# A unit's result turned in eight pieces on VectorE and laid out through DRAM, and the maxima's rounding two exponentials later

## The chip, the cores and the metric

The kernel runs on one core of a Trainium2 chip. The metric is the device time of one execution in microseconds. An execution taken with the hardware profiler gives the trace that the prediction reads; its times are counted from the start of the profiled span.

## The reference

One transformer layer: attention with 16 heads over 4096 tokens of width 256, then a gated feed-forward part, each followed by a residual sum and a layer norm. The change concerns the attention alone:

```python
B, N, d = x.shape            # 1, 4096, 256
h = H                        # 16
dk = d // h                  # 16
proj = quant4(x) @ ternary_weight(Wqkv_w).T + Wqkv_b
q = proj.reshape(B, N, h, dk).transpose(0, 2, 1, 3)
k = proj.reshape(B, h, N, dk)
v = proj.reshape(B, h, N, dk)
q, k = (rotary(q, N), rotary(k, N))
ql, kl = (q @ U, k @ U)
att = jnp.einsum('bhnr,bhmr->bhnm', ql, kl) / math.sqrt(dk)
y = jax.nn.softmax(att, axis=-1) @ v
y = y.transpose(0, 2, 1, 3).reshape(B, N, d)
return quant4(y) @ ternary_weight(Wo_w).T
```

## The kernel before, in words

**Units and steps.** The attention is cut into 64 units. A unit is a pair of heads and a block of 512 queries; the 4096 keys are passed in 32 tiles of 128, one tile to a step. The softmax needs the largest score of every query before any exponential, so each unit is gone through twice: first `largest` (L468 to L486) multiplies queries with keys and keeps only maxima, and 40 steps later (`LAG` = 32 + 8) `weights` (L511 to L519) multiplies again, with the maximum subtracted by a first matmul of `minus` and `m_rows`, and takes the exponential on ScalarE. `values` (L533) multiplies the exponentials of two steps with the values, in eight matmuls, four column strips of 32 running together, into the PSUM tile `av` of 128 x 512: per head of the pair two strips, one for even and one for odd key tiles, each with 16 value columns and one column that sums the exponentials. So in any step one unit's maxima, another's exponentials and a third's values are worked on side by side.

**The order.** Instructions stand in the order in which the program emits them; each engine and each DMA queue takes its own in that order. A loop over steps `s` first calls what was registered for the step with `at(step, f)`, then for odd `s` `largest(s)` and `weights(s - LAG)`, for even `s` `weights(s - LAG)` and `largest(s)`. `values` comes at odd steps, ahead of `largest`. On TensorE a pair of steps is therefore: eight `av` matmuls, two L468 matmuls, four score matmuls (L511), four more, two L468 matmuls.

**PSUM.** `ps_1` has three banks of 128 x 512. Each step of `largest` takes two of them, and VectorE frees each with one reduction of 512 columns (L476). Every other small use takes a bank of the same three: the turning of the queries (`query_steps`, L439), the preparing of the keys (L361, L367, L393), the projections (L139, L147), and the turning of a finished unit (L553). The scores have two double banks (`ps_sc`), `av` has one.

**A unit's maxima.** At a unit's last step of `largest`, VectorE reduces the 128 x 64 collected maxima to `m` (L481), ScalarE rounds them to a first part (L485) and GpSimd subtracts for the second (L486), all emitted inside `largest`, ahead of `weights` of the same step. Two steps on, `largest_rows` turns them on VectorE (L492), stores them to `m_dram` (L497) and loads them as rows (L500), both on SP's queue. They are needed when the unit's exponentials begin. Counted from the unit's first step of `largest`, its last is step 31, the turning step 34, the first exponential step 40.

**A unit's end.** `finish(u, 0)` copies `av` to SBUF on ScalarE (L548). Four steps later `finish(u, 1)` turns it in four fp32 transposes on TensorE into a `ps_1` bank (L553), VectorE adds the two strips of each head (L557), takes the reciprocal of the sums (L564), multiplies (L566), and SP stores the 512 x 32 result to `y_dram` (L572). After the last unit the feed-forward stage begins; its first VectorE operation (L737) splits the turned tokens, and its weights `h2` and `w3` are loaded on GpSimd's queue, emitted after the loop of steps.

GpSimd prepares queries and keys (L329 to L334, L431, L432), and from the ninth unit on rounds the weights for a check (L594, L595).

Of the kernel before, what the change touches and what calls it, by code (L numbers as in the profile page):

```python
# [9 lines left out]
F32 = mybir.dt.float32  # L10
# [4 lines left out]
ALU = mybir.AluOpType  # L15
AX = mybir.AxisListType
PSUM = bass.MemoryType.PSUM

P = 128
# [3 lines left out]
DK = D // H  # L23
HALF = DK // 2
NT = N // P
QB = 512
NQB = N // QB
NKT = N // P
DH = 1024
NC = DH // P  # L30
BT = 4
# [6 lines left out]
def attn_ffn_kernel(  # L38
# [22 lines left out]
    nc = tc.nc  # L61
# [6 lines left out]
    ident = const.tile([P, P], F32, name="ident")  # L68
# [11 lines left out]
    dram = ctx.enter_context(tc.tile_pool(name="dram", bufs=1, space=bass.MemoryType.DRAM))  # L80
# [157 lines left out]
    with ExitStack() as actx:  # L238
# [16 lines left out]
        m_parts = big.tile([P, 2, 2, 2, BT], F32R, name="m_parts")  # L255
        m_turned = big.tile([P, 32], F32, name="m_turned")
        m_rows = [big.tile([P, QB], F32R, name=f"m_rows{i}") for i in range(2)]
        m_dram = [dram.tile([32, P], F32, name=f"m_dram{i}") for i in range(2)]

        qpool = actx.enter_context(tc.tile_pool(name="qpool", bufs=2))  # L260
# [3 lines left out]
        ps_1 = actx.enter_context(tc.tile_pool(name="ps_1", bufs=3, space=PSUM))  # L264
# [185 lines left out]
        NU = (H // 2) * NQB  # L450
        LAG = NKT + 8
        AVLAG = 4
        kTs, qTs, mxs, avs, probs = {}, {}, {}, {}, {}
        todo = {}

        def at(step, f):
            todo.setdefault(step, []).append(f)

        def largest(s):

            u, i = divmod(s, NKT)
            qt, ck = divmod(i, NKT // BT)
            if i == 0:
                mxs[u] = stat.tile([P, BT, 2, NKT // BT], F32, name="mx")
            ps = [ps_1.tile([P, 512], F32, name="ps1") for j in range(2)]
            for j in range(2):
                rows = slice(64 * j, 64 * j + 64)
                nc.tensor.matmul(  # L468
                    ps[j],
                    lhsT=qTs[u][rows, ts(qt, P)],  # L470
                    rhs=kTs[u // NQB][rows, ts(ck, 512)],
                    start=True,
                    stop=True,
                )
            for j in range(2):
                nc.vector.tensor_reduce(  # L476
                    mxs[u][:, qt, j, ck : ck + 1], ps[j], AX.X, ALU.max
                )
            if i == NKT - 1:
                m = stat.tile([P, 2, BT], F32, name="m")  # L480
                nc.vector.tensor_reduce(  # L481
                    m, mxs.pop(u).rearrange("p t j c -> p j t c"), AX.X, ALU.max
                )
                parts = m_parts[:, 0]
                nc.scalar.copy(parts[:, :, 0, :], m)  # L485
                nc.gpsimd.tensor_tensor(  # L486
                    parts[:, :, 1, :], m, parts[:, :, 0, :].bitcast(F32), ALU.subtract
                )

        def largest_rows(u):  # L490

            nc.vector.transpose(  # L492
                m_turned, m_parts.bitcast(F32).rearrange("p a j k t -> p (a j k t)")
            )

            rows = m_dram[u % 2]
            nc.sync.dma_start(out=rows.rearrange("r (b c) -> b r c", b=4), in_=m_turned)  # L497
            rows = rows[: 4 * BT].rearrange("(j k t) c -> j k (t c)", j=2, k=2)
            for j in range(2):
                nc.sync.dma_start(  # L500
                    out=m_rows[u % 2][64 * j : 64 * j + 2, :].bitcast(F32), in_=rows[j]
                )
# [19 lines left out]
        def values(s):  # L522

            u, kt = divmod(s, NKT)
            pair = u // NQB
            if kt == 0:
                avs[u] = ps_av.tile([P, QB], F32, name="av")
            for j in range(2):
                for k in range(2):
                    a, c = divmod(kt + k, H)  # L530
                    strip = 32 * (2 * j + k)

                    nc.tensor.matmul(  # L533
                        avs[u][strip : strip + 32, :],
                        lhsT=v_all[
                            :, 2 * (2 * pair + j) + a, c * (DK + 1) : c * (DK + 1) + 32
                        ],
                        rhs=probs[s + k][:, j, :],
                        start=(kt == 0),
                        stop=(kt == NKT - 2),  # L540
                    )
            del probs[s], probs[s + 1]

        def finish(u, part, state={}):
            pair, qb = divmod(u, NQB)
            if part == 0:
                state[u] = qpool.tile([P, QB], F32, name="ya")
                nc.scalar.copy(state[u], avs.pop(u))  # L548
                return
            ya = state.pop(u)  # L550
            ps = ps_1.tile([P, 512], F32, name="ps1")
            for t in range(BT):
                nc.tensor.transpose(ps[:, ts(t, P)], ya[:, ts(t, P)], ident)  # L553

            both = ps.rearrange("p (n k e) -> p n k e", k=2, e=32)[:, :, :, : DK + 1]
            y = qpool.tile([P, BT, 2, DK + 1], F32, name="y")
            nc.vector.tensor_reduce(  # L557
                y.rearrange("p t j e -> p (t j) e"),
                both.rearrange("p n k e -> p n e k"),
                AX.X,  # L560
                ALU.add,
            )
            den = stat.tile([P, BT, 2], F32, name="den")
            nc.vector.reciprocal(den, y[:, :, :, DK])  # L564
            yu = stat.tile([P, BT, 2, DK], F32, name="yu")
            nc.vector.tensor_tensor(  # L566
                yu,
                y[:, :, :, :DK],
                den.unsqueeze(3).broadcast_to([P, BT, 2, DK]),
                ALU.mult,  # L570
            )
            nc.sync.dma_start(  # L572
                out=y_dram[qb].rearrange("(t p) d -> p t d", p=P)[
                    :, :, pair * 32 : (pair + 1) * 32
                ],
                in_=yu.rearrange("p t j e -> p t (j e)"),
            )
# [33 lines left out]
        with tc.manual_schedule():  # L611
# [32 lines left out]
            for u in range(NU):  # L644
                pair, qb = divmod(u, NQB)
                if qb == 2 and pair + 1 < H // 2:
                    def start_keys(pair=pair, u=u):
                        kTs[pair + 1] = kpool.tile([P, N], F32R, name="kT")
                        steps = key_steps(pair + 1, kTs[pair + 1])
                        for i, f in enumerate(steps):  # L650
                            at(NKT * u + 40 + 6 * i, f)
                    at(NKT * u + 8, start_keys)

                def start_queries(u=u, pair=pair, qb=qb):
                    qTs[u] = qpool.tile([P, QB], F32R, name="qT", bufs=3)
                    natural, transposed = query_steps(pair, qb, qTs[u])
                    natural()
                    at(NKT * (u - 1) + 26 if u else 0, transposed)

                if u:  # L660
                    at(NKT * (u - 1) + (18 if u == 1 else 6), start_queries)
                else:
                    start_queries()
                base = NKT * u + LAG
                for kt in range(0, NKT, 2):
                    at(base + kt + 1 + AVLAG, lambda s=NKT * u + kt: values(s))
                at(NKT * (u + 1) + 2, lambda u=u: largest_rows(u))
                at(base + NKT + AVLAG - 1, lambda u=u: finish(u, 0))
                at(base + NKT + AVLAG + 3, lambda u=u: finish(u, 1))
            last = NKT * NU  # L670
            at(last - 240, lambda: load_weights(w1_sb, w1T, 0))
            w2_sb, h1_sb, h2_sb = [None, None], [None, None], [None, None]
# [22 lines left out]
                    at(last + 2 + i, f)  # L695

            at(last - 60, start_front)
            for s in range(NKT * NU + LAG + AVLAG + 6):
                while todo.get(s):
                    todo[s].pop(0)()  # L700

                if s < NKT * NU and s % 2:
                    largest(s)
                if 0 <= s - LAG < NKT * NU:
                    weights(s - LAG)
                if s < NKT * NU and not s % 2:
                    largest(s)
# [213 lines left out]
```

## Time and profile before

| | |
|---|---|
| median of three executions | 3770.27 us (3770.03 to 3770.37) |
| profiled execution | 3770.6 us |
| its span, and granted TensorE clock | 3768.8 us, 0.988 |
| attention stage, about | 113 to 3088 us of the span |
| one unit in the steady stretch (1553.39 to 1598.81) | 45.42 us: TensorE busy 45.03, VectorE 41.14, ScalarE 32.90, GpSimd 6.54 |
| L476, reduction of 512 columns on VectorE | 4096 times, 684 ns recorded |
| L553, transposes of a unit on TensorE | 256 times, 286 ns |
| L557, L564, L566 on VectorE | 431, 204 and 292 ns, 64 times each |
| L485 on ScalarE, L486 on GpSimd | 197 and 206 ns, 64 times each |
| ScalarE's wait for `m` before L485 | 112.8 us in 64 times |

An engine's busy time is the union of what it ran; recorded durations of neighbours overlap, so that starts are closer together than durations say. An idle stretch is put down to the event that came last before it ended. The chain of waits is followed back from the last instruction to what released it each time; what does not stand on it had time to spare.

### The profile page before, as it was taken

To read this page: it belongs to the slowest core of one execution; us is meant where nothing else is said; L and a number is where in the kernel's file an instruction comes from. 1 tells how busy PE (TensorE), PEld (TensorE's weight loads), DVE (VectorE), ACT (ScalarE), POOL (GpSimd) and SP (SyncE) were. 2 spreads that over 40 slices of the span, in tenths; PEclk is the share of its full clock that TensorE was granted. 3 is DMA by queue.
4 is the path that set the end of the run, shared out by engine and by line. 5 is a ranking of instruction groups with operands and counts; after the bars stand their busy time and mean duration, and the time that the engine had idled before them with its cause. 6 is when DMAs were issued, how large, how long until landed. Compare 5 with 4: busy or idle time off the path is not lost.

```text
span 3768.8 us, 61593 instructions
## 1 busy us (share of the span) xinstructions
PE 3688.5 (98%) x24651; PEld 2065.1 (55%) x24651; DVE 3041.0 (81%) x5254; ACT 2381.5 (63%) x2782; POOL 471.5 (13%) x840
## 2 busy tenths in 40 slices
PE   6999999999999999999999999999999999999998
PEld 3454445444444454445444544455445448888887
DVE  6988988899889988998899889988999945555544
ACT  1566777777777777777777777767777773333333
POOL 3342112111211121111011111100000000000000
PEclk6999999999999999999999999999999999999999
DMA  1000000000000000000000000000010020000000
GB/s 36 13 14 3 9 9 9 9 9 9 9 9 9 9 9 9 9 9 8 9 9 9 9 9 9 9 3 3 25 48 14 9 70 6 18 17 24 28 6 13
DMA packets 78072, 50.91 MB, mean 14 GB/s; under 512 B 52688, under 2 KB 72400, under 8 KB 77776
## 3 DMA queue, kind: packets, MB, share of 16 engines
q1 hardware_dynamic: 73952, 35.35, 3.5%
q0 software_dynamic: 3824, 11.54, 0.9%
q8 instruction: 195, 3.19, 0.3%
q14 instruction: 101, 0.83, 0.1%
HBM read 37.44 MB, written 9.44 MB: 12 GB/s over the span
## 4 chain that ended last, share of the span: by engine, by line
PE 89%; DVE 6%; ACT 3%; issue 1%; POOL 0%; DMA 0%; ACTq 0%; SPq 0%
PE av L533 25%; PE sc L511 23%; PE ps L468 19%; PE ps_mm L753 17%; DVE mx L476 5%; ACT pr L519 2%; PE ps L553 1%; PE ps L393 1%; PE ps L439 1%; DVE m L481 0%; PE ps L367 0%; PE ps L361 0%; PE ps L147 0%; DVE ma L119 0%; PE ps_mm L798 0%
## 5 line engine op out<-in xcount | busy, mean ns | idle before, releaser
L476 DVE TENSOR_REDUCE mx<-ps 128x1 f32<-128x512 f32 x4096 | 2564.2, 684 | 308.4 <-PE ps L468 280.2
L519 ACT ACTIVATE pr<-sc 128x1024 f32<-128x1024 f32 x2048 | 2003.9, 1023 | 755.4 <-PE sc L511 743.7
L533 PE MATMUL av<-pr,v_all 128*32 128x512 f32 x8192 | 1092.0, 605 | 0.0
L468 PEld LDWEIGHTS ps<-kT,qT 64*128 64x128 f32 x4096 | 549.1, 185 | 972.1 <-DVE mx L476 699.1
L468 PE MATMUL ps<-kT,qT 64*128 64x512 f32 x4096 | 1047.7, 470 | 14.0 <-DVE mx L476 7.9
L511 PE MATMUL sc<-m_rows,minus 64*128 64x512 f32 x4096 | 851.6, 409 | 16.2 <-ACT pr L519 12.2
L511 PE MATMUL sc<-qT,kT 64*128 64x512 f32 x4096 | 815.0, 391 | 0.0
L511 PEld LDWEIGHTS sc<-m_rows,minus 64*128 64x128 f32 x4096 | 392.5, 185 | 134.4 <-ACT pr L519 84.8
L511 PEld LDWEIGHTS sc<-qT,kT 64*128 64x128 f32 x4096 | 393.2, 185 | 74.1
L533 PEld LDWEIGHTS av<-pr,v_all 128*32 128x32 f32 x8192 | 161.6, 108 | 267.9 <-issue 266.7
L486 POOL TENSOR_TENSOR m_parts<-m,m_parts 128x8 fp32r<-128x8 f32 x64 | 13.2, 206 | 2233.4 <-ACT m_parts L485 2233.4
L786 ACT ACTIVATE gate<-ps_mm,sc_hs 128x512 f32<-128x512 f32 x128 | 88.1, 688 | 312.8 <-PE ps_mm L753 269.6
L735 DVE CAST h<-gate 128x512 fp32r<-128x512 f32 x128 | 54.4, 425 | 223.1 <-ACT gate L786 223.1
L737 DVE TENSOR_TENSOR h<-gate,h 128x512 fp32r<-128x512 f32 x192 | 132.3, 689 | 5.1
L753 PE MATMUL ps_mm<-h,h1a 128*128 128x512 f32 x512 | 128.9, 394 | 0.0
L753 PE MATMUL ps_mm<-h,h2a 128*128 128x512 f32 x512 | 127.2, 391 | 0.0
L753 PE MATMUL ps_mm<-h,h1b 128*128 128x512 f32 x512 | 126.5, 389 | 0.0
L753 PE MATMUL ps_mm<-h,h2b 128*128 128x512 f32 x512 | 126.5, 389 | 0.0
L778 DVE SCALAR_TENSOR_TENSOR gate<-ps_mm,sc_s,gate 128x512 f32<-128x512 f32 x64 | 48.0, 750 | 81.9 <-ACT gate L776 58.0
L753 PEld LDWEIGHTS ps_mm<-h,h1b 128*128 128x128 f32 x512 | 96.1, 188 | 20.1
L753 PEld LDWEIGHTS ps_mm<-h,h2b 128*128 128x128 f32 x512 | 96.1, 188 | 19.9
L753 PEld LDWEIGHTS ps_mm<-h,h2a 128*128 128x128 f32 x512 | 95.6, 188 | 19.6
(148 smaller groups left out, 1915.4 us busy)
## 6 DMA issues: line engine op xcount, KB each, us to landing
xs<-in_x SPq DMA_DIRECT2D x16, 512.0 KB
y_dram<-yu SPq DMA_DIRECT2D x64, 64.0 KB
xs<-in_h1T SPq DMA_DIRECT2D x8, 512.0 KB
xs<-in_h2T SPq DMA_DIRECT2D x8, 512.0 KB
yb<-y_dram SPq DMA_DIRECT2D x8, 512.0 KB
out<-xs SPq DMA_DIRECT2D x8, 512.0 KB
m_rows<-m_dram SPq DMA_DIRECT2D x128, 4.0 KB
h1a<-in_h1T POOLq DMA_DIRECT2D x2, 1024.0 KB, 6.4
```

Of the source, the lines that this page charges most:

```text
L393: nc.tensor.matmul(ps[:, ts(k, P)], lhsT=flat[:, ts(4 * i + k, P)], rhs=identr, start=True, stop=True,)
L439: nc.tensor.matmul(ps[:, ts(t, P)], lhsT=qq[:, t].rearrange("p j k e -> p (j k e)"), rhs=identr, start=True, stop=True,)
L468: nc.tensor.matmul(ps[j], lhsT=qTs[u][rows, ts(qt, P)], rhs=kTs[u // NQB][rows, ts(ck, 512)], start=True, stop=True,)
L476: nc.vector.tensor_reduce(mxs[u][:, qt, j, ck : ck + 1], ps[j], AX.X, ALU.max)
L511: nc.tensor.matmul(ps[:, j, :], lhsT=minus[rows, :] if first else kTs[u // NQB][rows, ts(kt, P)], rhs=m_rows[u % 2][rows, :] if first else ...
L519: nc.scalar.activation(pr, ps, AF.Exp)
L533: nc.tensor.matmul(avs[u][strip : strip + 32, :], lhsT=v_all[:, 2 * (2 * pair + j) + a, c * (DK + 1) : c * (DK + 1) + 32], rhs=probs[s + k ...
L735: eng(dst[:, k, 0, :], g)
L737: nc.vector.tensor_tensor(dst[:, k, 1, :], g, dst[:, k, 0, :].bitcast(F32), ALU.subtract)
L753: nc.tensor.matmul(ps, lhsT=sb[:, ks, ts(o, P)] if split else wo[:, k, :], rhs=src[:, k, i, :], start=(k == 0 and i == 0), stop=(k == n - ...
L778: nc.vector.scalar_tensor_tensor(g, pb, scales["s2"][:, o : o + 1], gate, ALU.mult, ALU.mult)
L786: nc.scalar.activation(g, ps, AF.Gelu, scale=scales[sc][:, o : o + 1])
```

## The change

The four transposes on TensorE go. The copy of `av` is turned by VectorE instead, which transposes within blocks of 32 x 32: eight calls of 64 columns, one at every second step. Four stores, one for each strip of 32 partitions, lay the blocks out in DRAM as 512 queries by four strips, and one load brings them back with the queries on partitions. GpSimd adds the two strips of each head and, after VectorE's reciprocal, multiplies. The store to `y_dram` stays as it was. For the last unit the eight calls follow each other in one step and the rest comes two steps later. The copies `ya`, `yt`, `y4` and `y` have one buffer each (`ya` and `y` had two).

The rounding of the maxima becomes a function of its own, `largest_parts`, called at the second step after `m`, so that two more exponentials stand ahead of it on ScalarE; `largest_rows` comes one step later than it did.

```diff
+        y_raw = [dram.tile([QB, 4, 32], F32, name=f"y_raw{i}") for i in range(2)]
...
                 nc.vector.tensor_reduce(
                     m, mxs.pop(u).rearrange("p t j c -> p j t c"), AX.X, ALU.max
                 )
-                parts = m_parts[:, 0]
-                nc.scalar.copy(parts[:, :, 0, :], m)
-                nc.gpsimd.tensor_tensor(
-                    parts[:, :, 1, :], m, parts[:, :, 0, :].bitcast(F32), ALU.subtract
-                )
+                ms[u] = m
+
+        def largest_parts(u):
+            parts, m = m_parts[:, 0], ms.pop(u)
+            nc.scalar.copy(parts[:, :, 0, :], m)
+            nc.gpsimd.tensor_tensor(
+                parts[:, :, 1, :], m, parts[:, :, 0, :].bitcast(F32), ALU.subtract
+            )
...
-        def finish(u, part, state={}):
+        def finish(u):
+            yas[u] = qpool.tile([P, QB], F32, name="ya", bufs=1)
+            nc.scalar.copy(yas[u], avs.pop(u))
+            yts[u] = qpool.tile([P, QB], F32, name="yt", bufs=1)
+
+        def turn(u, i):
+            nc.vector.transpose(yts[u][:, ts(i, 64)], yas[u][:, ts(i, 64)])
+
+        def gather(u):
+            del yas[u]
+            raw = y_raw[u % 2]
+            yt = yts.pop(u).rearrange("p (b e) -> p b e", e=32)
+            for strip in range(4):
+                nc.sync.dma_start(
+                    out=raw.rearrange("(b q) s e -> s q b e", q=32)[strip],
+                    in_=yt[32 * strip : 32 * strip + 32],
+                )
+            y4s[u] = qpool.tile([P, BT, 2, 2, 32], F32, name="y4", bufs=1)
+            nc.sync.dma_start(
+                out=y4s[u].rearrange("p t j k e -> p t (j k e)"),
+                in_=raw.rearrange("(t p) s e -> p t (s e)", p=P),
+            )
+
+        def add_strips(u):
+            y4 = y4s.pop(u)
+            ys[u] = qpool.tile([P, BT, 2, DK + 1], F32, name="y", bufs=1)
+            nc.gpsimd.tensor_tensor(
+                ys[u], y4[:, :, :, 0, : DK + 1], y4[:, :, :, 1, : DK + 1], ALU.add
+            )
+
+        def divide(u):
             pair, qb = divmod(u, NQB)
-            if part == 0:
-                state[u] = qpool.tile([P, QB], F32, name="ya")
-                nc.scalar.copy(state[u], avs.pop(u))
-                return
-            ya = state.pop(u)
-            ps = ps_1.tile([P, 512], F32, name="ps1")
-            for t in range(BT):
-                nc.tensor.transpose(ps[:, ts(t, P)], ya[:, ts(t, P)], ident)
-
-            both = ps.rearrange("p (n k e) -> p n k e", k=2, e=32)[:, :, :, : DK + 1]
-            y = qpool.tile([P, BT, 2, DK + 1], F32, name="y")
-            nc.vector.tensor_reduce(
-                y.rearrange("p t j e -> p (t j) e"),
-                both.rearrange("p n k e -> p n e k"),
-                AX.X,
-                ALU.add,
-            )
+            y = ys.pop(u)
             den = stat.tile([P, BT, 2], F32, name="den")
             nc.vector.reciprocal(den, y[:, :, :, DK])
             yu = stat.tile([P, BT, 2, DK], F32, name="yu")
-            nc.vector.tensor_tensor(
+            nc.gpsimd.tensor_tensor(
                 yu,
...
-                at(NKT * (u + 1) + 2, lambda u=u: largest_rows(u))
-                at(base + NKT + AVLAG - 1, lambda u=u: finish(u, 0))
-                at(base + NKT + AVLAG + 3, lambda u=u: finish(u, 1))
+                at(NKT * (u + 1) + 1, lambda u=u: largest_parts(u))
+                at(NKT * (u + 1) + 3, lambda u=u: largest_rows(u))
+                end = base + NKT + AVLAG - 1
+                at(end, lambda u=u: finish(u))
+                gap = 2 if u < NU - 1 else 0
+                for i in range(8):
+                    at(end + 2 + gap * i, lambda u=u, i=i: turn(u, i))
+                at(end + 2 + 8 * gap, lambda u=u: gather(u))
+                at(end + 4 + 11 * gap, lambda u=u: add_strips(u))
+                at(end + 4 + 12 * gap, lambda u=u: divide(u))
...
-            for s in range(NKT * NU + LAG + AVLAG + 6):
+            for s in range(NKT * NU + LAG + AVLAG + 4):
```

`base` is `NKT * u + LAG`, so `end` is odd. Counted in steps of the 32-step frame in which they fall, the eight pieces stand at steps 13, 15 and so on to 27, the stores and the load at 29, the sum at 5 of the next frame, the reciprocal and the product at 7; the rounding stands at step 1 and the turning of the maxima at step 3 (steps 33 and 35, counted from the unit's first).

More of the change, by code (lines that the diff above doesn't have):

```diff
@@ L452, in attn_ffn_kernel @@
         AVLAG = 4
-        kTs, qTs, mxs, avs, probs = {}, {}, {}, {}, {}
+        kTs, qTs, mxs, ms, avs, probs = {}, {}, {}, {}, {}, {}
+        yas, yts, y4s, ys = {}, {}, {}, {}
         todo = {}
```

## The prediction

> **What bounds the kernel now.** I read the busy shares and the costliest groups first, then the chain of waits over two units of the attention stage, then the VectorE timeline beside it. The page names TensorE:
>
> ```profile
> PE 3688.5 (98%) x24651; PEld 2065.1 (55%) x24651; DVE 3041.0 (81%) x5254; ACT 2381.5 (63%) x2782; POOL 471.5 (13%) x840
> ```
>
> The 98% doesn't say how much of it is held up, so the chain decides. Its columns are start us, us, what. First the place where a finished unit is turned on TensorE (L553):
>
> ```profile
> 1569.87 0.43 PE ps L468 x2
> 1570.30 0.94 PE sc L511 x8
> 1571.24 0.34 PE ps L468 x2
> 1571.58 0.99 PE av L533 x8
> 1572.58 0.47 PE ps L468 x2
> 1573.05 1.29 DVE mx L476 x2
> 1574.34 0.04 issue
> 1574.38 0.66 PE ps L553 x4
> 1575.04 0.99 PE av L533 x8
> ...
> 1577.75 0.99 PE av L533 x8
> ```
>
> An `av` burst of eight matmuls marks a pair of key tiles (two steps). Burst to burst takes 2.71 us (1575.04 to 1577.75), but 3.46 us (1571.58 to 1575.04) where L553 stands: the transposes wait for a PSUM bank that VectorE still reads, and then run. Second, the place where a unit's maxima are finished:
>
> ```profile
> 1551.92 0.99 PE av L533 x8
> 1552.92 0.48 PE ps L468
> 1553.39 1.29 DVE mx L476 x2
> ...
> 1554.70 0.23 DVE m L481
> ...
> 1555.01 0.04 ACT m_parts L485
> ...
> 1556.03 1.02 ACT pr L519
> ...
> 1557.10 0.73 PE sc L511 x4
> 1557.84 0.23 PE ps L468 x2
> 1558.06 0.99 PE av L533 x8
> ```
>
> Two pairs take 6.14 us here instead of 5.41: ScalarE's copy L485 waits for `m` and keeps back exponentials that are ready, and TensorE then waits for their score banks. From one `m` to the next the unit takes 45.42 us (1553.39 to 1598.81 in the same view): 16 pairs of 2.705 are 43.28, these two places add 0.75 and about 0.71, and a third place, the query transposes L439, adds 0.67 and stays. Third, what VectorE does inside the plain pairs (start, us, engine and operation, idle before and its releaser):
>
> ```profile
> 1554.70 0.22 DVE L481 TENSOR_REDUCE m<-mx 128x8 f32<-128x64 f32 x1
> 1554.84 2.54 DVE L476 TENSOR_REDUCE mx<-ps 128x1 f32<-128x512 f32 x4
> ...
> 1562.23 2.48 DVE L476 TENSOR_REDUCE mx<-ps 128x1 f32<-128x512 f32 x4 [0.22 <-PE ps L468]
> 1564.93 2.48 DVE L476 TENSOR_REDUCE mx<-ps 128x1 f32<-128x512 f32 x4 [0.21 <-PE ps L468]
> ```
>
> Four reductions fill 2.48 of 2.70 us, and some 0.22 us are idle, always just before the first of the four. Consecutive reductions start 0.60 us apart though each is recorded with 0.68; so the slot from the fourth one's turn to the next pair's first is 2.70 - 4 x 0.60 = 0.30 us. And `m`, with 64 columns, keeps its successor back only 0.14 us (1554.70 to 1554.84).
>
> [...] The trace shows a granted clock of 0.51 in the 3.5 us from 3067.5, after TensorE had waited 3.01 us for an exponential.
>
> **The change part by part.**
>
> *Turning leaves TensorE.* Four transposes and the bank they take go, and with them the VectorE reduction (431 ns) and product (292 ns) that ran in the same pair. That pair falls from 3.46 to 2.71: 0.75 us in each of 62 units (the trace's sum over them is 46.7 us). The first such place and the last unit's are not in the steady loop.
>
> *Eight pieces on VectorE.* A 128x64 transpose isn't in the trace; the nearest is the 128x32 one:
>
> ```profile
> L492 DVE STREAM_TRANSPOSE m_turned<-m_parts x64: 201/202/212, 99.9 to 3036.3; 128x32 f32<-128x32 f32 x64
> ```
>
> In the timeline its successor starts 0.12 us after it (99.92, then 100.04). [...] Each piece is issued at an odd step ahead of that step's reductions, which is exactly the 0.30 us slot, one piece to a pair. It waits for `ya` at most once, and the copy (1569.99, 0.59 us) is done two microseconds before. Taken: nothing. Bounds: not below nothing, since no other instruction becomes shorter; above, if a piece held everything back for its full 0.235 us after the fourth reduction's recorded end (1564.71), the next would start at about 1565.00 instead of 1564.93: 0.07 x 8 x 63 = 35 us. A delay there counts in full: the first reduction's end frees the bank that TensorE's next L468 takes 0.05 us later (1565.62, 1565.67). The reciprocal (204 ns, before the reductions of step +7) has the same slot. In the first five units, VectorE also carries projection work in the same pairs: I charge 2 us in all (0 to 4).
>
> *Layout through DRAM.* Four stores and one load on SP. An issue takes 0.38 us (`y_dram`), and SP's round trip for `m_dram` was 1.99 us (issued 1557.53, next DMA at 1559.52). Stores: 3 x 0.38 + 2.0, plus some 0.2 for 512 pieces instead of 128: about 3.4 us; load 2.2, GpSimd sum of 136 columns 0.48 (between L329's 325 ns for 64 and L334's 738 for 256): about 6 us. The last piece is at step 27, the sum is due at step 37 and the reciprocal at step 39: 12 steps of 1.35, 16 us. Queued behind the load on SP is the next `m_dram`, now at step 35, 10.8 us after the last piece; SP is free 3.4 us after it. Hidden, in steady state. GpSimd's extra work (0.48 + 0.46 us a unit) lies in 13% busy.
>
> *Rounding of the maxima.* The copy moves to step 33, behind the exponentials of steps 31 and 32. ScalarE then has 0.77 us idle in each pair, `m` is 0.9 us old, the copy takes 0.2: nothing waits. What is next late: VectorE's `m` shifts two reductions by 0.26 us, still in time for the bank (TensorE's L468 in that pair started on time in the trace, at 1555.56). Saved: 0.68 to 0.74 a unit; I take 0.71 x 58 = 41 us and 1 us for the first six, where projections overlap. The rows leave one step later. Transpose to landing was about 4 us (1557.30, with the loads issued by 1560.06 and some 1.2 to land); now it starts at about 1558.5 in that frame and `m_rows` are wanted by step 40's scores at about 1564.5: 2 us spare. If that were lost, each microsecond late would cost 64 us.
>
> *The end.* The last unit has no pairs to hide in. Before, the copy of `ya` ended at 3090.58 and the first VectorE operation of the feed-forward stage ran at 3093.19. Now: eight pieces 1.3 us, stores, load and sum 6 us, then the reciprocal, behind which that operation is queued: 3098, so 4.8 us later. TensorE idles for it[...]: 6.5 us, once (0 to 10). The big weight loads on GpSimd's queue are now behind the sum: they don't disturb the small transfers, and they start ten microseconds late, against some 40 us until `h2` is used.
>
> Sum: 46.7 + 42 - 2 - 6.5 = 80 us. The profiled execution took 3770.6 us (span 3768.8 and 1.8 around it), the median of three is 3770.27: for both, about **3690 us**.
>
> **Rivals.** (1) *The pieces don't fit.* If each delays its pair by 0.07 to 0.15 us, 35 to 76 us are given back: 3725 to 3766. For it: the reductions that follow are on the tight bank loop. Against: the successor 0.12 us after L492. (2) *The maxima's stall moves instead of going*, the rows or their copy becoming the new wait: only 46.7 - 8.5 = 38 us saved, 3732. Against: 0.77 us idle in ScalarE and 2 us spare for the rows. (3) *Slower: the small stores hold SP's queue.* 2048 pieces of 128 bytes a unit; if a 32-partition store ran on few DMA engines it would land late, and SP would wait with `m_dram` behind the load. Up to 10.8 + 2 = 12.8 us after the last piece this costs nothing, then each microsecond costs 63 us; from 14.1 us on the change is slower. [...] For it: no such transfer in the trace. Against: a 64 KB `y_dram` store of 512 such pieces is never waited for[...].
>
> **How the numbers follow.** As forecast, hidden pieces and both stalls gone: 0.78, own range 3680 to 3702. Rival 1: 0.08. Rival 2: 0.06. Rival 3: 0.08. The range runs from 3680 to 3715, which takes in a few hundredths of a microsecond per piece; some 2 in 10 is outside. About 0.2% (7.5 us) is what can be told from no change. Faster: the forecast, rival 2 and most of rival 1, 0.88; within: 0.03; slower: rival 3 and the tail of rival 1, 0.09.
>
> **What would show it.** In the changed profile the bursts of L533's successor should stand 2.71 us apart at both places and a unit should take 43.96 us; VectorE's idle 0.22 us should shrink where pieces lie, with the reductions still 2.70 apart; ScalarE's wait for `m` (112.8 us) should be gone; and a gap of 5 to 7 us should stand before the feed-forward stage. Reductions 2.75 us apart in eight pairs would mean rival 1; SP waiting for `y_raw` and score matmuls late at the unit's start, rival 3.

## The result and the profile after

The changed kernel takes 3703.16 us (median of 6, 3702.46 to 3703.56) against 3770.15 us for the kernel before (median of 6): a ratio of 0.9823, 95% interval 0.9810 to 0.9835. It is faster by 67 us, 1.8%. The direction and the range of the forecast hold; it had promised 80. The profiled execution has a span of 3701.1 us, 67.7 below the 3768.8 of before.

The page's chain by engine before the change, then the lines of the changed kernel's page that answer to those shown of before:

```profile
PE 89%; DVE 6%; ACT 3%; issue 1%; POOL 0%; DMA 0%; ACTq 0%; SPq 0%
```

```profile
PE 3627.2 (98%) x24395; PEld 2055.8 (56%) x24395; DVE 3066.4 (83%) x5638; ACT 2384.5 (64%) x2782; POOL 525.0 (14%) x968
...
PE 97%; DVE 2%; ACT 0%; DMA 0%; POOL 0%; issue 0%; SPq 0%; DVEq 0%; ACTq 0%; POOLq 0%
...
L559 DVE STREAM_TRANSPOSE yt<-ya 128x64 f32<-128x64 f32 x512 | 119.0, 234 | 18.8 <-ACT ya L553 18.8
```

TensorE is 98% busy in both kernels, and yet one is 67 us shorter: its share of busy time could not have told. The chain tells it. It is now 97% TensorE where it was 89%, because the two detours over VectorE and ScalarE in each unit are gone. In the chain of waits of one unit (start us, us, what), the burst of value matmuls at step 13 and its successor, where the result was turned before, and those at steps 33 and 35, where the maxima held ScalarE up:

```profile
2792.35 1.00 PE av L538 x8
...
2795.04 0.99 PE av L538 x8
...
2820.08 1.00 PE av L538 x8
...
2822.79 0.99 PE av L538 x8
```

Both distances are 2.7 us; they were 3.46 and about 3.4. VectorE's timeline in three pairs (start, us, engine and operation, idle before):

```profile
2799.21 2.49 DVE L478 TENSOR_REDUCE mx<-ps 128x1 f32<-128x512 f32 x4
2801.61 0.23 DVE L559 STREAM_TRANSPOSE yt<-ya 128x64 f32<-128x64 f32 x1
2801.92 2.48 DVE L478 TENSOR_REDUCE mx<-ps 128x1 f32<-128x512 f32 x4
2804.32 0.23 DVE L559 STREAM_TRANSPOSE yt<-ya 128x64 f32<-128x64 f32 x1
2804.63 2.48 DVE L478 TENSOR_REDUCE mx<-ps 128x1 f32<-128x512 f32 x4
```

A piece starts 0.60 us after the fourth reduction's start (2799.21 + 4 x 0.60) and the next reductions follow 0.31 us after it, 2.71 after the ones before: the idle 0.22 us that stood there is filled, and no pair is longer. ScalarE's timeline at the maxima:

```profile
2819.36 1.94 ACT L524 ACTIVATE pr<-sc 128x1024 f32<-128x1024 f32 x2 [0.76 <-PE sc L516]
2821.19 0.20 ACT L490 CAST m_parts<-m 128x8 fp32r<-128x8 f32 x1
2822.09 1.94 ACT L524 ACTIVATE pr<-sc 128x1024 f32<-128x1024 f32 x2 [0.70 <-PE sc L516]
```

The copy follows the exponentials without an idle gap, and the next exponentials wait for TensorE (0.70 us), not for the copy. ScalarE's wait for `m`, before and after (us in total, times, longest):

```profile
ACT m_parts L485 <- DVE m L481: 112.8, 64, 7.0
```

```profile
ACT m_parts L490 <- DVE m L483: 7.0, 1, 7.0
```

The one that is left is the first unit's.

Over all units, by the distances from the start of one burst to the next in both traces: the place of the result gains 47.7 us, the place of the maxima 39.2, all other places lose 3.6 together, and the way to the first burst is 0.8 shorter. That is 84.1 us up to the last burst. From there to the end the kernel before took 680.3 us, the changed one 696.6: **16.3 us are given back once, at the end of the attention.** The chain of waits there:

```profile
3005.94 0.59 ACT ya L553
...
3006.56 1.14 DVE yt L559 x8
...
3007.71 0.32 SPq L567
...
3009.40 10.17 DMA y_raw<-yt
...
3019.71 2.87 DMA y<-y_raw
...
3022.73 0.48 POOL y L580
...
3023.23 0.22 DVE den L589
...
3023.97 0.70 DVE xT L769
```

From the first store's issue (3007.71) to the landing of the last (3019.57) it takes 11.9 us; the prediction had 3.4. GpSimd's timeline says what else was on its way:

```profile
3003.95 1.48 POOL L171 DMA_DIRECT2D h2a<-in_h2T  x2 [15.71 <-PE sc L516]
3006.21 1.43 POOL L171 DMA_DIRECT2D h2b<-in_h2T  x2 [0.78 <-PE av L538]
...
3007.63 1.45 POOL L171 DMA_DIRECT2D w_sb<-in_w3T  x2
...
3022.73 0.47 POOL L580 TENSOR_TENSOR y<-y 128x136 f32<-128x136 f32 x1 [13.65 <-DMA y<-y_raw]
```

The loads of `h2` and half of `w3` are issued before the last unit's sum L580, although the source has them after it. TensorE, whose work is queued behind VectorE's L769, and that behind the reciprocal L589, stands for 16.25 us:

```profile
3007.96 0.50 PE L785 MATMUL ps_mm<-xT,w_sb 128*128 128x512 f32 x1 [0.29 <-ACT xT L767]
...
3024.72 1.65 PE L785 MATMUL ps_mm<-xT,w_sb 128*128 128x512 f32 x3 [16.25 <-DVE xT L769]
```

### The profile page after: what moved, and what is told of

Its sections match the earlier page's. It is cut to its first block, busy times and chain, and to the rows that moved or that the text cites. A ratio compares the mean times of both kernels' runs of the same rounds, so it can differ in the third digit from the quotient of the medians.

```text
span 3701.1 us, 62137 instructions
## 1 busy us (share of the span) xinstructions
PE 3627.2 (98%) x24395; PEld 2055.8 (56%) x24395; DVE 3066.4 (83%) x5638; ACT 2384.5 (64%) x2782; POOL 525.0 (14%) x968
## 4 chain that ended last, share of the span: by engine, by line
PE 97%; DVE 2%; ACT 0%; DMA 0%; POOL 0%; issue 0%; SPq 0%; DVEq 0%; ACTq 0%; POOLq 0%
PE av L538 27%; PE sc L516 27%; PE ps L470 21%; PE ps_mm L785 17%; PE ps L394 1%; PE ps L440 1%; DVE mx L478 1%; PE ps L368 1%; PE ps L147 0%; DMA y_raw<-yt 0%; PE ps L362 0%; DVE ma L119 0%; PE ps_mm L830 0%; ACT pr L524 0%; PE ps_mm L147 0%
## 5 line engine op out<-in xcount | busy, mean ns | idle before, releaser
L470 PEld LDWEIGHTS ps<-kT,qT 64*128 64x128 f32 x4096 | 557.7, 185 | 968.8 <-DVE mx L478 747.4
L516 PE MATMUL sc<-m_rows,minus 64*128 64x512 f32 x4096 | 842.7, 404 | 4.0 <-ACT pr L524 3.6
L769 DVE TENSOR_TENSOR h<-gate,h 128x512 fp32r<-128x512 f32 x192 | 132.3, 689 | 5.1
L559 DVE STREAM_TRANSPOSE yt<-ya 128x64 f32<-128x64 f32 x512 | 119.0, 234 | 18.8 <-ACT ya L553 18.8
```

Source lines behind the costliest of these rows:

```text
L470: nc.tensor.matmul(ps[j], lhsT=qTs[u][rows, ts(qt, P)], rhs=kTs[u // NQB][rows, ts(ck, 512)], start=True, stop=True,)
L516: nc.tensor.matmul(ps[:, j, :], lhsT=minus[rows, :] if first else kTs[u // NQB][rows, ts(kt, P)], rhs=m_rows[u % 2][rows, :] if first else ...
L559: nc.vector.transpose(yts[u][:, ts(i, 64)], yas[u][:, ts(i, 64)])
L769: nc.vector.tensor_tensor(dst[:, k, 1, :], g, dst[:, k, 0, :].bitcast(F32), ALU.subtract)
```

## The experiments

Theory A: the steady state is as forecast, and the shortfall lies at the end, where the weight loads share the DMA engines with the last unit's small stores. Its rivals: the trip through DRAM takes this long by itself (B), or small delays are spread over the units. Times are medians in us, each with the ratio to the kernel before, measured beside it.

| run | time | ratio, 95% interval |
|---|---|---|
| last unit turned on TensorE | 3684.65 | 0.9772 (0.9755 to 0.9788) |
| weight loads behind the last sum | 3691.72 | 0.9792 (0.9776 to 0.9809) |
| rounding alone | 3734.96 | 0.9904 (0.9888 to 0.9921) |
| turning alone | 3740.95 | 0.9921 (0.9904 to 0.9937) |
| pieces twice | 3731.43 | 0.9897 (0.9880 to 0.9913) |
| pieces three times | 3848.70 | 1.0211 (1.0194 to 1.0228) |
| rows two steps later | 3726.39 | 0.9884 (0.9868 to 0.9901) |
| rounding behind one exponential | 3685.53 | 0.9777 (0.9761 to 0.9794) |
| stores twice | 3685.82 | 0.9775 (0.9758 to 0.9791) |
| stores six times | 3977.84 | 1.0555 (1.0538 to 1.0573) |

**The last unit turned on TensorE.**

```diff
-                gap = 2 if u < NU - 1 else 0
+                if u == NU - 1:
+                    at(end + 4, lambda u=u: finish_on_pe(u))
+                    continue
+                gap = 2
```

`finish_on_pe` is what `finish(u, 1)` was before, four transposes on TensorE, reduction, reciprocal and product on VectorE, and the store.

> The last unit alone is turned on TensorE, as in the kernel before; all other units as in the changed kernel. If the changed kernel's shortfall lies at the end of the attention alone (the first feed-forward operation of VectorE waits behind the last unit's reciprocal for the trip through DRAM), the stretch after the last burst of value matmuls falls from 696.6 us back to about 680.3 and the time from 3703 to about 3687 us. If the end were not the place (small delays spread over the units), it stays within 3 us of 3703.

Measured: 3684.65 us, 18.5 below the changed kernel. The stretch after the last burst is 680.48 us, as before the change, which accounts for 16.2 of them; 1.3 more lie between the last unit's own bursts. So the end is the place, and this version beats both kernels: it keeps the gain of 63 units and doesn't pay at the one that has nothing to hide in.

**The weight loads behind the last sum.**

```diff
-        for i in range(2):
-            load_weights(h2_sb[i], h2T, i * NC // 2)
-        load_weights(w3_sb, w3T, 0)
...
+            if split:
+                for i in range(2):
+                    load_weights(h2_sb[i], h2T, i * NC // 2)
+                load_weights(w3_sb, w3T, 0)
             transpose_x(0)
```

> The loads of h2 and w3 are issued after the branch that opens the feed-forward stage, so on GpSimd's queue they stand behind the last unit's sum and product. Theory A, the loads crowd out the last unit's stores: without them the stores and the load take about 6 us instead of 15, TensorE's gap before the feed-forward stage falls from 16.25 us to about 6, and the time to about 3693 us. Theory B, the trip through DRAM takes this long by itself: the gap stays at about 16 us and the time at 3703 or, with the loads late, above.

Measured: 3691.72 us. The chain of waits at the end:

```profile
3005.42 0.32 SPq L567
...
3006.86 2.00 DMA y_raw<-yt
...
3009.00 2.79 DMA y<-y_raw
...
3011.93 0.49 POOL y L580
...
3013.17 0.70 DVE xT L766
```

First issue to last landing is now 3.4 us (3005.42 to 3008.86), as the prediction had it, TensorE's gap is 7.7 us instead of 16.25, and the stretch after the last burst is 687.9 us: 7.6 more than before instead of 16.3. Theory A holds, B falls. Of the 16.3 us, 8.7 come from the loads ahead of the stores and 7.6 from the trip itself, with the pieces and the lower clock that go with it (0.987 granted over this execution, 0.988 with the last unit on TensorE).

**Each part alone.** The first edit is the kernel before with `largest_parts` and the two changed due steps; the second is the changed kernel without them, of which this is a part:

```diff
-                at(NKT * (u + 1) + 1, lambda u=u: largest_parts(u))
-                at(NKT * (u + 1) + 3, lambda u=u: largest_rows(u))
+                at(NKT * (u + 1) + 2, lambda u=u: largest_rows(u))
```

> The kernel before with the rounding of the maxima placed as in the changed one (copy and difference at step 33, turning at step 35), and the result still turned on TensorE. If the two stalls are independent, the pairs at the maxima fall to 2.71 us, those at the result stay at 3.46, and 39 to 42 us are saved: about 3729 us. If the stall of one is only covered by the other (both wait for the same banks), less than 30 us.

> The changed kernel with the rounding of the maxima back where it stood before (inside the last step of the maxima, turned two steps later). If the two parts add up: the changed kernel's 3703 plus about 41 us, 3744 us; the pairs at the result at 2.71, those at the maxima at about 3.4. If turning on VectorE disturbs the maxima (or helps them), it differs from that by more than 5 us.

Measured: 36 us saved by the rounding alone, 30 by the turning alone, together 66: they add up to the change's 67. The median distances of the bursts, from the starts in the traces, and as the unit the sum of the medians of its 16 distances:

| | at the result | at the maxima | unit |
|---|---|---|---|
| before | 3.46 | 3.44 | 45.45 |
| rounding alone | 3.46 | 2.70 | 44.71 |
| turning alone | 2.70 | 3.44 | 44.70 |
| both | 2.70 | 2.71 | 43.97 |

Turning alone carries the same end (696.4 us), so 47 us less 16. Which share of its 0.75 us belongs to the transposes and which to the VectorE reduction and product that ran beside them was not tried. Rounding alone came out some 3 us short of its range. Its trace shows where: in three units (the 56th, 58th and 59th) the pair of steps 39 and 41 is 1.3 to 1.5 us longer. There the last byte of `m_rows` came 6.7 to 6.9 us after the turning began instead of the usual 3.5 to 3.8. In the kernel before the same three units show 6.4 to 6.5, and the earlier turning covered it. In those units GpSimd issues weight loads of 1.5 or 2 MB about a microsecond after the turning (`h1` at 2735.66 and 2781.62 us, the turnings at 2734.7 and 2780.7), so the rows travel while the loads do; that this is the cause was not tried by itself. The changed kernel speaks for it: there the same loads are issued 6 us after the turning (2698.08 after 2692.04 and 2742.04 after 2736.01), behind GpSimd's new product L591, and the rows of these units take 3.7 to 3.8 us. That the change as a whole doesn't pay this is luck, since the prediction doesn't count these loads.

**How full VectorE's slot is.** From here on the base is the version with the last unit on TensorE. Two repetitions, then three in a second run:

```diff
-            nc.vector.transpose(yts[u][:, ts(i, 64)], yas[u][:, ts(i, 64)])
+            for _ in range(2):
+                nc.vector.transpose(yts[u][:, ts(i, 64)], yas[u][:, ts(i, 64)])
```

> Base: the version with the last unit turned on TensorE (3684.65 us). Every one of the eight pieces is turned twice, into the same place. If VectorE has a slot of 0.30 us in each pair and a piece takes 0.15 of it, two pieces just fit: 0 to 10 us more, pairs at 2.71 to 2.73. If a piece in truth already filled the slot, each second one costs its 0.15 us in 8 pairs of 63 units, 75 us.

> The same base, every piece turned three times: 3 x 0.145 = 0.44 us against a slot of 0.30. The third piece should delay the next reduction by about 0.14 us, and with it the bank and the pair: 0.14 x 8 x 63 = 70 us more, about 3755, the eight pairs at about 2.85 us. If VectorE's delay doesn't reach TensorE (the banks have slack that the slot doesn't show), less than 20 us.

Measured: 47 and 164 us more. Both are above my ranges, and VectorE's timeline shows why, first of the doubled pieces and then of the tripled:

```profile
1510.07 0.52 DVE L560 STREAM_TRANSPOSE yt<-ya 128x64 f32<-128x64 f32 x2
1510.51 2.45 DVE L478 TENSOR_REDUCE mx<-ps 128x1 f32<-128x512 f32 x4
1512.88 0.51 DVE L560 STREAM_TRANSPOSE yt<-ya 128x64 f32<-128x64 f32 x2
```

```profile
1534.46 0.79 DVE L560 STREAM_TRANSPOSE yt<-ya 128x64 f32<-128x64 f32 x3
1535.17 2.45 DVE L478 TENSOR_REDUCE mx<-ps 128x1 f32<-128x512 f32 x4
1537.54 0.79 DVE L560 STREAM_TRANSPOSE yt<-ya 128x64 f32<-128x64 f32 x3
```

A repeated piece does not overlap with the one before it: it starts 0.26 to 0.28 us later, and only the last leaves the way free after 0.17. In the trace the repeated piece, which writes the same place, has a wait for the semaphore that the earlier piece raises, and no other instruction of the pair has such a wait. The eight pieces of the last unit in the changed kernel, which go to different places and have no such wait, start 0.13 us apart from the second on. Two thus take 0.43 to 0.44 us (1510.07 to 1510.51), three 0.71, and the pairs grow to 2.80 and 3.08. The size of the slot follows from them: what fills VectorE less what the pair grows, 0.43 - 0.10 and 0.71 - 0.37, is 0.33 to 0.34 us both times. A single piece's 0.17 us is half of it. The second theory of each run (the slot already full, or no effect on TensorE) is refuted; my sums for the runs were wrong in what a repeated piece costs.

**How much time the rows have.**

```diff
-                at(NKT * (u + 1) + 3, lambda u=u: largest_rows(u))
+                at(NKT * (u + 1) + (5 if u < NU - 1 else 3), lambda u=u: largest_rows(u))
```

> The same base, the maxima turned and sent two steps later (step 37 instead of 35; the last unit as it was). In the changed kernel's trace the last byte of the rows arrives 3.5 to 3.8 us after the turning begins and the first scores that need them are due some 6 us after it: about 2 us spare. A pair later takes 2.7 us: about 0.6 us late in each of 62 units, 20 to 45 us more, in the pair of steps 39 to 41. If the rows had no part in the time (more than 2.7 us spare), nothing.

Measured: 42 us more, in the traces 39 of it in one place: the pair of steps 39 to 41 has 3.37 us in the median instead of 2.71. The chain now runs over the rows:

```profile
1542.54 1.94 DMA m_dram<-m_turned
...
1544.54 1.38 DMA m_rows<-m_dram
...
1546.05 0.93 PE sc L516 x4
```

2.7 us later costs 0.66: 2.0 us were spare in the base.

**The rounding behind one exponential.**

```diff
-                at(NKT * (u + 1) + 1, lambda u=u: largest_parts(u))
+                at(NKT * (u + 1), lambda u=u: largest_parts(u))
```

> The same base, the rounding called one step earlier, so that one more exponential stands ahead of it instead of two. The maxima are ready about when that exponential ends; if only the wait for them cost the time, the copy then costs no more than its 0.2 us out of 0.77 idle: within 5 us of 3684.65. If a copy between the two exponentials of a pair holds TensorE's scores up, 0.2 us x 63: 13 us more.

Measured: 3685.53 us, no difference. One exponential ahead of the copy is enough; what cost the time was only that ScalarE waited for `m`.

**How many small stores SP's queue bears.** Further sets of the four stores, one and then five, go to tiles that nothing reads, ahead of the unit's own:

```diff
+            for more in y_more:
+                for strip in range(4):
+                    nc.sync.dma_start(
+                        out=more.rearrange("(b q) s e -> s q b e", q=32)[strip],
+                        in_=yt[32 * strip : 32 * strip + 32],
+                    )
```

> Base: the version with the last unit turned on TensorE (3684.65 us). Every unit's four stores are made twice (the first set into a tile of its own that nothing reads), eight stores ahead of the load on SP's queue. In the changed kernel's trace the trip took 4.2 us to the load's issue and SP then stood idle for 6.2 us before the next store of maxima. Four more stores take 2 to 3 us: no change, within 5 us of 3684.65. If the small pieces already hold up SP or the DMA engines, up to 63 x 2.5 = 160 us more.

> The same with six sets, 24 stores: about 24 x 0.6 us of issue and 2 of landing, SP free some 16 to 17 us after the last piece, 5 to 6 us late for the maxima's store; 2 us of that are spare, so 3 to 4 us late in each of 62 units: 190 to 250 us more, about 3900, slower than the kernel before, and TensorE waiting for the rows of maxima. If the stores don't hold the queue (the load's wait doesn't keep the maxima's store back), it stays near 3685.

Measured: nothing for two sets, 293 us more for six. SP's timeline in the second run:

```profile
1633.95 11.55 SPq L569 DMA_DIRECT2D y_more<-yt  x20
1645.55 2.16 SPq L574 DMA_DIRECT2D y_raw<-yt  x4
1649.21 0.38 SPq L579 DMA_DIRECT2D y<-y_raw  x1
1649.68 0.53 SPq L503 DMA_DIRECT2D m_dram<-m_turned  x1
1652.37 0.57 SPq L506 DMA_DIRECT2D m_rows<-m_dram  x2
```

The maxima's store follows the load at once: it was ready and queued. The rival that ended slower than before is a real mechanism; the change itself stays well on this side of it. The price was more than I expected (190 to 250 us): 221 of the 293 us lie in the pairs of steps 39 to 41, as much as expected, but 64 in the pairs that follow them and 6 behind the last burst, and the granted clock fell from 0.988 to 0.957.

## Why the prediction came out as it did

**The result's turning: right.** 0.75 us in each unit was forecast, 0.76 is measured in the steady units, 47.7 us against 46.7 in all.

**The pieces on VectorE: right.** Taken at nothing, and nothing is seen: 234 ns recorded against 235, successor free after 0.17 (in the runs with repeated pieces) against 0.15, in a slot of 0.33 against 0.30. An estimate from the trace of before gives both forecast figures: a reduction kept its successor back for 0.60 us with 512 columns and for 0.14 us with 64, which is 1.03 ns for each column more, and 32 columns more than the 202 ns and 0.12 us of L492 make 235 ns and 0.15 us. Measured, 32 more columns lengthen the record from 202 to 234 ns. The freeing of the successor grew by 0.05 us, more than the 0.03 of that estimate. The bound that a piece costs 0.07 us was not needed.

**The layout through DRAM in the steady state: right.** SP issues the load 3.6 us after the first store in the median unit (3.4 to 5.1) against 3.4, and then stands idle until the maxima's store. A slower unit, with 4.2 us and 6.2 us idle:

```profile
2813.47 2.64 SPq L567 DMA_DIRECT2D y_raw<-yt  x4
2817.65 0.38 SPq L572 DMA_DIRECT2D y<-y_raw  x1
2824.18 0.53 SPq L502 DMA_DIRECT2D m_dram<-m_turned  x1
```

How many DMA engines a store of 32 partitions uses isn't shown in the traces, and how little the prediction gave its third rival was its author's estimate. The time was measured: in the unit above the first packet of 128 bytes begins at 2814.32 us, 0.85 after the first store's issue, and the last of the 2048 ends at 2817.23, 3.8 after it.

**The rounding: right, a little too large.** 39.2 us against 42. I had counted what two neighbouring pairs lose in one unit; in every other unit 0.15 us of that stands in the pair ahead of the maxima and is there after the change too (the mean of that pair is 2.90 us in both traces).

**The end: the step that failed.** The prediction put it at 6.5 us with the words "The big weight loads on GpSimd's queue are now behind the sum: they don't disturb the small transfers". They were ahead of it. I read the order of the source as the order of the queue, as the description of the kernel does; on GpSimd's queue the loads stand ahead of the last sum. They are emitted outside the stretch whose order is written by hand. In the run that put them behind the sum they stand inside such a stretch and behind the branch as well; which of the two fixed their place was not tried. With them really behind it, the end cost 7.6 us against 6.5, so the rest of that sum (pieces, trip, clock) was nearly sound. Of the 6.5 us, 4.8 are VectorE's later start; the other 1.7 agree with an estimate for the clock from the trace of before, where 0.51 was granted for 3.5 us: 0.49 of 3.5. The load took 2.8 us where the author's estimate was 2.2, and from the reciprocal to the first operation of the next stage another 0.7 us pass. A warning stood in the trace of before, where those loads are issued as soon as the last scores end:

```profile
3088.00 1.47 POOL L171 DMA_DIRECT2D h2a<-in_h2T  x2 [32.36 <-PE sc L511]
```

The DMA share (packet time over the time of all DMA engines; up to 1.24 in the stretches below) is 1.01 over the next 12 us: a stretch in which small transfers had to be priced as shared until their order was known.

In the changed kernel the granted clock dropped there (stretch, its length, busy time of each engine, then clock, DMA share and GB/s):

```profile
3008.00:3012.00 4.00, 0.47 (x1) 0.15 (x1) 0.00 (x0) 1.68 (x2) 1.08 (x2) 0.86 1.14 406
3012.00:3016.00 4.00, 0.00 (x0) 0.00 (x0) 0.00 (x0) 0.00 (x0) 0.00 (x0) 0.50 1.24 419
3024.00:3028.00 4.00, 3.28 (x8) 2.61 (x9) 1.26 (x2) 0.69 (x1) 1.03 (x2) 0.51 0.90 177
```

It is 0.50 while TensorE waits and 0.51 in the first four microseconds after it resumes. The 0.86 of the first stretch puts the drop near 3010.9 us (an estimate: half a clock for 28% of it), 2.4 us after TensorE's last matmul ended (3008.46).

VectorE's first operation of the stage starts 19.5 us after the last burst instead of 4.7: 14.8 of the 16.3 us. The rest goes with the clock of 0.51: of the stage's large matmuls the second starts 14.8 us later than before, counted from the last burst, the tenth 16.2, and it stays at that.

By terms, in us, forecast then measured: result -46.7, -47.7; maxima -42, -39.2; other places +2, +3.6; start 0, -0.8; end +6.5, +16.3; sum -80, -67.7. The end makes up 9.8 of the 12.5 us between the two sums.

Among the other places is one that I overlooked: in the last unit the rows' turning, one step later, falls behind VectorE's first work on the next stage, which is due at step 34: it starts at 2956.82 us, 5.4 us after `m` (2951.39). Its exponentials begin 0.9 us late, of which 0.4 comes back in the next pair. Another 1.3 us lie between the last unit's value bursts, where the clock of this execution stood at half for 6.8 us (2980.2 to 2987.0) instead of the 3.4 of before (3067.6 to 3071.0); in the runs above that time is anything from none to 6.8, so it isn't put down to the change.

## What to carry to other kernels

Here work went on a nearly full engine (41.14 of 45.42 us busy in a unit before) for nothing, cut into pieces smaller than the slot (0.17 us in 0.33) that its wait for another engine leaves in each round, and placed just ahead of the instruction that waits; take the slot from the starts (0.60 us apart), not from recorded durations (0.68). Treat the last round by itself: what was hidden in all others was bare there, and a waiting instruction ahead of the next stage held back all of it (16.3 us at its end). Read a queue's order from the built program or the trace: here loads that the source has behind the last sum were issued ahead of it.

## What the hardware showed that was not expected

Beside large packets, small ones moved at about the large ones' pace: the last unit's four stores, 256 KB in packets of 128 bytes, took 11.9 us beside the weight loads and 3.4 us without them, at about the same place in the program. The packets in the trace went about one for one: from 3012 to 3016 us 412 small ones began beside 396 of 4 KB, and from 3017 to 3018, where the loads' packets had 1 KB, 339 beside 329; without the loads up to 915 began in a microsecond. Before that, the first small packet began 3.5 us after its store was issued, instead of 0.85. And a VectorE transposition of 128x64 that waits for the one before it started 0.26 us after it, where eight in a row without such a wait started 0.13 us apart from the second on.
